# A four-layer graph network on one core: degrees counted inside the sort's pair product, records taken apart within the first convolution, one-hots that read a one from PSUM

## The chip, the cores and the metric

One core of a Trainium2 chip runs the whole program. The metric is the device time of one execution in microseconds (us), as the median of ten runs. Below, PE is the tensor engine (PEld its weight loads), DVE the vector engine, ACT the scalar engine, POOL the GpSimd engine, SP the sync engine, which here only issues transfers. L12 is line 12 of the kernel before.

## The reference, cut to what matters

12,500 nodes with 16 features, 400,000 edges that come sorted by destination in the host's arrays (the kernel sorts them anew, by source and destination bucket). Four layers follow each other, each on `h = relu(layernorm(x))`, and each is added to `x`:

```
deg  = segment_sum(1, dst) + 1 ;  dinv = 1/sqrt(deg)
L0:  two GCN convolutions: out = dinv * (segment_sum((dinv*h)[src], dst) + dinv*h), weights and relu between
L1:  relational messages: W_rel[type[e]] applied to h[src], times an edge score, summed over dst
L2:  edge network: messages from h[src] and 4 edge attributes, summed over dst, divided by max(count, 1), batch norm
L3:  a non-linear coupling of h[src] and h[dst] with the edge weight, summed over src
```

Every layer needs rows gathered by `src` and sums over `dst`. What matters here is how many edges each node has as destination (`deg`), which node of its bucket each edge names (`src & 127`, `dst & 127`), and which type it has.

## The kernel before, in words

**Buckets and groups.** Nodes lie as 98 buckets of 128. The kernel sorts edges into records of 8 words (source low bits, destination low bits, destination bucket and type packed in word 0; edge score, weight, four attributes) so that edges of one (destination bucket, source bucket) pair stand together in granules of G = 9. A group is 128 granules, one a partition; there are NG = 512 groups, of which the first MAIN_S = 396 are in use for these inputs in source order. The rest runs only under a condition (`tc.If` in `in_steps`) that does not hold here.

**Histogram.** One product per 128 edges counts the pairs; from the counts come the start of each pair (`cbase`) and the tables `mvx`, `here`, `spare` from which each granule's place in the destination order (`place`) is made.

**Sort (L455 to L611).** 125 blocks of 3200 edges, 25 columns of 128. For each column: ACT copies the running counts `p_c` to `c_sb` (L573), PE adds this column's pair product, `ohd` by `ohs`, to `p_c` (L574), and PE looks up each edge's start with `ohdt` and `c_sb` (L576, `p_l`). DVE counts equal keys before each edge in its column (L579), picks the edge's own start (L583, L584), and after the 25 columns makes the slots (L589 to L601). POOL scatters the block's 25 columns of records `q` with one indirect transfer each (L603). `q` has two buffers, so a block's `q` is written when the scatter of two blocks before has landed. The degrees have their own products (L475, `count_degrees`): a one-hot `ohl` of the destination's low bits is made after the loop (L586), and the products of `ohd` with it are issued in the next block's program. `ohdt` (L516) is made with `scalar_tensor_tensor` and a column of ones held in PSUM (`fixed`, `one_p`).

**Taking apart (L612 to L690).** After the sort, for all 512 groups: load the records (`rt`, 60 groups at a time), extract source low bits (`slo`), destination low bits (`dl0`), type (`typ`), bucket (`dhi`) on DVE; transpose them on PE and write them as rows to DRAM (`srow`, `trow`, `hrow`, L641 to L660). Then, 35 groups at a time, load `hrow` back to 98 partitions (`hb`), make a one-hot `ht` (L669), multiply with `mvx` (L672), and make `place` with eight small operations (L676 to L687). `dl0` is stored to DRAM and loaded again at L882.

**Convolutions (L889 to L931).** Run twice. Steps of two groups (`in_steps`: `fetch` of one step is issued ahead of `rows` of the step before). Each four groups (LD), `fetch` loads a row block (SP) and makes a one-hot of 4608 columns on DVE (L700, `one_hot_t`: `tensor_scalar` with `is_equal`): in the first convolution the source one-hot `o` from `srow`, which is also stored to `oh_s`; in the second `o` is loaded from `oh_s`, and the type one-hot `ot` from `trow` is made and stored to `oh_t` for layer 1. ACT issues these loads and stores. `rows`: 18 products with the bucket's rows (L919), a copy to `msg` on ACT (L923), in the first convolution a copy of `dl0` beside it on DVE (L925), and two indirect transfers by POOL (L715, `send`), which put each granule in its place of `buf1` or `buf2`. `msg` has six buffers, `o` and `ot` three each, `pg` three. A `sum_pass` in destination order follows each convolution.

**Layer 2 (L1081 to L1115).** Per step: products, a multiplication `q` (L1095) on DVE, a folding of `q` (L1102), and two additions: on POOL `m + q0` (L1104), on DVE `m + q1` (L1105). Then the message is split in three bf16 parts (L245 to L249, ACT and DVE), and POOL sends it.

The order on each engine is fixed when the program is built; an engine takes its instructions in that order.

Of the kernel before, what the change touches and what calls it, by code (L numbers as in the profile page):

```python
# [30 lines left out]
F32 = mybir.dt.float32  # L31
BF16 = mybir.dt.bfloat16
# [12 lines left out]
P = 128  # L45
# [22 lines left out]
LD = 4  # L68
S = UN * G
# [12 lines left out]
def gnn_kernel(  # L82
# [186 lines left out]
    with ExitStack() as begin:  # L269
        base = begin.enter_context(tc.tile_pool(name="base", bufs=1))  # L270
        parts, n = 8, 4
        e1 = base.tile([P, NG * G // parts // n, R], F32, name="e1")
        nc.vector.memset(e1, 0.0)
        nc.vector.memset(e1[:, :, 0:1].bitcast(I32), EMPTY)
        v = rec.rearrange("p (k n s) -> k p n s", k=parts, n=n)
        for k in range(parts):
            nc.scalar.dma_start(v[k], e1.rearrange("p s r -> p (s r)")[:, None, :]
                                .to_broadcast([P, n, NG * G // parts // n * R]))
        w = (NG - MAIN_D) // 4
        for k in range(MAIN_D, NG, w):  # L280
            nc.scalar.dma_start(buf4.rearrange("(p g) c -> p g c", g=NG)[:, k : k + w],
                                zeros[:, None, : G * F].to_broadcast([P, w, G * F]))

        deg_b = base.tile([NB, P], F32, name="deg_b")
        cbase = base.tile([NB, NB], F32, name="cbase")
        mvx = base.tile([NB, NG, 3], BF16, name="mvx")
        n_d = base.tile([P, NB], F32, name="n_d")
        v_d = base.tile([P, NB], F32, name="v_d")
        spare = base.tile([P, NG], F32, name="spare")
        rank_e = base.tile([P, NG], F32, name="rank_e")  # L290
        here = base.tile([P, NG], F32, name="here")
        here_i = base.tile([P, NG], I32, name="here_i")
        nc.gpsimd.iota(here_i, pattern=[[P, NG]], base=0, channel_multiplier=1)
        nc.vector.tensor_copy(here, here_i)

        def one_hot_n(out, v2, n, iota=iota_b):

            nc.vector.tensor_tensor(out.rearrange("p k (m t) -> p k m t", t=2),  # L298
                                    v2[:, :, None, :].to_broadcast([P, v2.shape[1], n // 2, 2]),
                                    iota[:, None, :n].rearrange("p a (m t) -> p a m t", t=2)  # L300
                                    .to_broadcast([P, v2.shape[1], n // 2, 2]), op=ALU.is_equal)


        with tc.tile_pool(name="hist", bufs=2) as hist, tc.tile_pool(name="hpsum", bufs=1, space=PSUM) as ps:
            p_cnt = ps.tile([NB, NB], F32, name="p_cnt")
            clear(p_cnt, NB, NB)
            for it in range(NBE // UE):
                e0 = it * UE * BE
                hi = {}
                for name, idx in (("d", dst), ("s", src)):  # L310
                    v = hist.tile([P, UE, KE], I32, name="v" + name)
                    nc.sync.dma_start(v, idx[e0 : e0 + UE * BE].rearrange("(u p k) -> p u k", u=UE, k=KE))
                    v = v.rearrange("p u k -> p (u k)")
                    t = hist.tile([P, KI], I32, name="t" + name)
                    nc.vector.tensor_scalar(t, v, 7, None, op0=ALU.logical_shift_right)
                    hi[name] = hist.tile([P, KI, 2], BF16, name="hi" + name)
                    nc.vector.tensor_copy(hi[name], t[:, :, None].to_broadcast([P, KI, 2]))
                key = hist.tile([P, KI], F32, name="key")
                nc.vector.scalar_tensor_tensor(key, hi["d"][:, :, 0], float(NB), hi["s"][:, :, 0],
                                               op0=ALU.mult, op1=ALU.add)  # L320
                hd = hist.tile([P, KI], F32, name="hd")
                nc.scalar.copy(hd, hi["d"][:, :, 0])
                for v, row, dt in ((key, keyrow, F32), (hd, drow, BF16)):
                    pt = ps.tile([KI, P], F32, name="pt", bufs=2)
                    nc.tensor.transpose(pt, v, ident)
                    tt = hist.tile([KI, P], dt, name="tt" + row.name[-8:])
                    nc.scalar.copy(tt, pt)
                    nc.sync.dma_start(row[it * KI : (it + 1) * KI, :], tt)
                for u in range(UE):
                    sl = slice(u * KE, (u + 1) * KE)  # L330
                    ohd = hist.tile([P, KE, NB], BF16, name="ohd")
                    one_hot_n(ohd, hi["d"][:, sl, :], NB)
                    ohs = hist.tile([P, KE, NB], BF16, name="ohs")
                    one_hot_n(ohs, hi["s"][:, sl, :], NB)
                    for k in range(KE):
                        nc.tensor.matmul(p_cnt, ohd[:, k, :], ohs[:, k, :], start=False, stop=False,
                                         skip_group_check=True)
            cnt = base.tile([NB, NB], F32, name="cnt")
            nc.vector.tensor_copy(cnt, p_cnt)


        with tc.tile_pool(name="bw", bufs=1) as bw, tc.tile_pool(name="bpsum", bufs=1, space=PSUM) as ps:

            def up(v, shape, by, name):

                f = bw.tile(shape, F32, name=name)
                nc.vector.tensor_scalar(f, v, 1.0 / by, (by - 1) / by - 0.45, op0=ALU.mult, op1=ALU.add)
                nc.vector.tensor_scalar(f, f, MAGIC, MAGIC, op0=ALU.add, op1=ALU.subtract)
                return f

            def up128(v, shape, name):
                i = bw.tile(shape, I32, name=name + "_i")
                nc.vector.tensor_scalar(i, v, float(P - 1), None, op0=ALU.add)
                nc.vector.tensor_scalar(i, i, 7, None, op0=ALU.logical_shift_right)
                f = bw.tile(shape, F32, name=name)
                nc.vector.tensor_copy(f, i)
                return f

            def over_groups(lhsT, v):

                m = lhsT.shape[1]
                p = ps.tile([P, 1024], F32, name="p_g")
                for c in range(0, NG, 512):
                    w = min(512, NG - c)
                    nc.tensor.matmul(p[:m, c : c + w], lhsT, v[:, c : c + w], start=True, stop=True)
                return p[:m, :NG]

            sq = [NB, NB]
            n = up(cnt, sq, G, "n")
            tri = before[:NB, :NB]  # L370
            p_pre = ps.tile(sq, F32, name="p_pre")
            nc.tensor.matmul(p_pre, tri, n, start=True, stop=True)
            p_all = ps.tile(sq, F32, name="p_all")
            nc.tensor.matmul(p_all, ones[:NB, :NB], n, start=True, stop=True)
            tg = up128(p_all, sq, "tg")
            incl = bw.tile(sq, F32, name="incl")
            nc.vector.tensor_tensor_scan(incl, ones[:NB, :NB], tg, 0.0, op0=ALU.mult, op1=ALU.add)
            nc.vector.tensor_sub(incl, incl, tg)
            gs = bw.tile(sq, F32, name="gs")
            nc.vector.scalar_tensor_tensor(gs, incl, float(P), p_pre, op0=ALU.mult, op1=ALU.add)  # L380
            nc.vector.tensor_scalar(cbase, gs, float(G), None, op0=ALU.mult)
            p_ts = ps.tile([NB, 1], F32, name="p_ts")
            nc.tensor.matmul(p_ts, n, ones[:NB, 0:1], start=True, stop=True)
            td = bw.tile([NB, 1], F32, name="td")
            nc.vector.tensor_reduce(td, n, axis=AX.X, op=ALU.add)

            group_i = bw.tile([NB, NG], I32, name="group_i")
            nc.gpsimd.iota(group_i, pattern=[[1, NG]], base=0, channel_multiplier=0)
            group = bw.tile([NB, NG], F32, name="group")
            nc.vector.tensor_copy(group, group_i)  # L390
            ts = bw.tile([NB, 1], F32, name="ts")
            nc.vector.tensor_copy(ts, p_ts)
            first, ends = [], []
            for name, t, bkt in (("s", ts, bkt_s), ("d", td, bkt_d)):
                c = up128(t, [NB, 1], "c" + name)
                p_f = ps.tile([NB, 1], F32, name="p_f", bufs=2)
                nc.tensor.matmul(p_f, tri, c, start=True, stop=True)
# [901 lines left out]
```

## Time and profile before

| what | value |
|---|---|
| median of 10 runs | 11687.88 us (11679.14 to 11690.1) |
| the profiled execution: its own time | 11684.19 us |
| the profiled execution: span, first to last instruction | 11682.2 us |
| busy share of the span | DVE 79%, POOL 67%, PE 59%, PEld 55%, ACT 22% |
| POOL: scatter of the sort, 3125 indirect transfers | 3030.2 us busy, 970 ns each |
| POOL: sends of convolutions and layer 2, 1188 | 1601.6 us busy, 1348 ns each |
| DVE: one-hots of the two convolutions, 2 x 99 | 260.3 + 260.1 us, 2630 ns each |

The program is a sequence of stages with different limits, so a share over the whole span says little; each stage is read by itself. Busy time of POOL for an indirect transfer is the making of its descriptors; the transfer itself runs on the DMA engines afterwards. A "releaser" behind an idle time names what ended the wait. The granted clock of PE is given with each window as a share of full speed.

### The profile page before, as it was taken

The numbers are of one execution on the slowest core, as the hardware profiler recorded it, in microseconds if no ns is written. First come the engines' busy times: TensorE is split into PE (matmuls) and PEld (weight loads), VectorE is DVE, ScalarE is ACT, GpSimd is POOL, SyncE is SP. The second block draws the span as 40 slices with busy tenths as digits, with TensorE's granted clock in tenths as the row PEclk, the third lists the DMA queues.
The fourth block names the chain that finished last, engine by engine and source line by source line (L and its number), as shares of the span: only waits on it lengthen the run. The fifth ranks groups of instructions, "written<-read, shape, count | busy, mean of one in ns | idle before, by whom it ended". The sixth has DMA issues, their size and how long they took to land. (4 is left out here: it accounts for less than half of the span.)

```text
span 11682.2 us, 284671 instructions
## 1 busy us (share of the span) xinstructions
PE 6925.5 (59%) x112895; PEld 6383.5 (55%) x112895; DVE 9234.3 (79%) x17851; ACT 2551.9 (22%) x7316; POOL 7803.4 (67%) x8668
## 2 busy tenths in 40 slices
PE   5655555555555552225622578888867655656776
PEld 5555555555555552224422467777766555546766
DVE  8877877787877775448433899999999788955999
ACT  0122112222112221221222100000046322011555
POOL 0277777777777773884388369999999587300776
PEclk7555555555555555555555589999975799555555
DMA  3344444444444435775488533333334466456443
GB/s 102 96 137 132 132 125 136 137 137 132 132 132 136 137 112 175 238 238 171 125 270 271 167 104 106 103 104 105 101 115 132 122 202 186 152 155 205 138 127 113
DMA packets 1100970, 1704.98 MB, mean 146 GB/s; under 512 B 660792, under 2 KB 727909, under 8 KB 1080779
## 3 DMA queue, kind: packets, MB, share of 16 engines
q1 hardware_dynamic: 746151, 737.61, 21.4%
q10 hardware_dynamic: 164704, 715.37, 18.7%
q0 software_dynamic: 188704, 233.01, 6.3%
q8 instruction: 907, 14.86, 0.5%
q14 instruction: 504, 4.13, 0.1%
HBM read 1079.99 MB, written 555.86 MB: 140 GB/s over the span
## 5 line engine op out<-in xcount | busy, mean ns | idle before, releaser
L603 POOL DMA_INDIRECT rec<-q,slot x3125 | 3030.2, 970 | 1012.9 <-issue 950.7
L576 PE MATMUL p_l<-c_sb,ohdt 98*128 98x98 f32 x6250 | 1875.3, 457 | 242.8 <-DVE gran L591 193.6
L715 POOL DMA_INDIRECT buf<-msg,place x1188 | 1601.6, 1348 | 497.6 <-issue 227.7
L576 PEld LDWEIGHTS p_l<-c_sb,ohdt 98*128 98x128 f32 x6250 | 1634.2, 323 | 323.9 <-issue 318.8
L574 PE MATMUL p_c<-ohs,ohd 128*98 128x98 bf16 x3125 | 817.9, 262 | 1172.8 <-DVE ohs L298 1124.8
L769 DVE TENSOR_TENSOR oh<-lo,row 128x2304 bf16<-128x2304 bf16 x1070 | 1409.4, 1342 | 72.6 <-ACT lo L756 44.1
L1007 PE MATMUL pw<-wt,ot 128*128 128x256 bf16 x10692 | 1235.5, 273 | 263.6 <-DVE pr L1011 244.0
L1007 PEld LDWEIGHTS <-ot 128*128 128x128 fp8e4 x10692 | 1044.8, 98 | 431.3 <-issue 312.5
L574 PEld LDWEIGHTS <-ohd 128*98 128x98 bf16 x3125 | 626.2, 200 | 1134.0 <-DVE ohd L298 971.1
L573 ACT COPY c_sb<-p_c 98x98 f32<-98x98 f32 x3125 | 756.9, 242 | 1488.1 <-PE p_c L574 1476.2
L747 PE MATMUL pg<-xg,o 128*128 128x16 bf16 (+1 forms) x33156 | 947.3, 173 | 204.7 <-DVE o L700 152.5
L747 PEld LDWEIGHTS <-o 128*128 128x128 fp8e4 x33156 | 922.4, 101 | 221.6 <-DVE o L700 164.5
L1011 DVE TENSOR_TENSOR pr<-pw,hg 128x1536 f32<-128x1536 f32 x594 | 1020.2, 1743 | 7.0 <-ACT hg L751 3.9
L919 PE MATMUL pg<-xg,o 128*128 128x48 bf16 x7128 | 324.7, 215 | 1084.4 <-DVE o L700 502.7
L579 DVE SCALAR_TENSOR_TENSOR junk<-keyb,key,fixed 128x128 bf16<-128x128 f32 x3125 | 916.7, 340 | 0.0
L715 POOL DMA_INDIRECT buf<-mm,place x396 | 834.2, 2107 | 121.2 <-issue 67.4
L919 PEld LDWEIGHTS <-o 128*128 128x128 fp8e4 x7128 | 296.6, 118 | 1112.5 <-DVE o L700 524.4
L786 PEld LDWEIGHTS <-oh 128*128 128x128 bf16 x22464 | 652.0, 104 | 432.3 <-DVE oh L769 241.3
L1216 POOL DMA_INDIRECT xj<-buf,place x396 | 396.1, 1000 | 625.4 <-ACT lo L756 539.1
L800 PE MATMUL pa<-m,oh 128*128 128x48 bf16 x11772 | 587.7, 215 | 361.3 <-DVE oh L769 338.8
L1023 DVE TENSOR_TENSOR pr<-pr 128x2304 f32<-128x2304 f32 (+1 forms) x396 | 783.7, 1979 | 0.1
L583 DVE TENSOR_TENSOR own<-p_l,ohs 128x490 f32<-128x490 f32 x625 | 418.1, 669 | 433.7 <-PE p_l L576 429.0
(362 smaller groups left out, 13322.5 us busy)
## 6 DMA issues: line engine op xcount, KB each, us to landing
o<-oh_s ACTq DMA_DIRECT2D x396, 576.0 KB
keyb<-keyrow ACTq DMA_DIRECT2D x125, 1600.0 KB
buf<-zeros SPq DMA_DIRECT2D x120, 1536.0 KB
m<-buf SPq DMA_DIRECT2D x218, 432.0 KB
db<-drow ACTq DMA_DIRECT2D x125, 612.5 KB
mf<-buf SPq DMA_DIRECT2D x109, 576.0 KB
er<-erow SPq DMA_DIRECT2D x109, 576.0 KB
t<-srow SPq DMA_DIRECT2D x99, 576.0 KB
```

The lines of the kernel that those rows point to most:

```text
L573: nc.scalar.copy(c_sb, p_c)
L574: nc.tensor.matmul(p_c, ohd[:, k, :], ohs[:, k, :], start=False, stop=False, skip_group_check=True)
L576: nc.tensor.matmul(p_l[:, k - kb, :], ohdt[:, k * P : (k + 1) * P], c_sb, start=True, stop=True)
L579: nc.vector.scalar_tensor_tensor(junk, keyb[:, k * P : (k + 1) * P], key[:, k : k + 1], earlier_p, op0=ALU.is_equal, op1=ALU.mult, accum_o ...
L603: st = nc.gpsimd.indirect_dma_start(out=rec_rows, out_offset=bass.IndirectOffsetOnAxis(ap=slot[:, k : k + 1], axis=0), in_=q[:, k, :], in_ ...
L715: st = nc.gpsimd.indirect_dma_start(out=buf, out_offset=bass.IndirectOffsetOnAxis(ap=place[:, g : g + 1], axis=0), in_=msg, in_offset=None)
L747: nc.tensor.matmul(pg[:, k, :], o[:, k * P : (k + 1) * P], xg[:, (g + k // G) % LD, c, :], start=c == 0, stop=c == 2)
L769: nc.vector.tensor_tensor(oh.rearrange("p k (m t) -> p k m t", t=2), lo2[:, v : v + S, None, :].to_broadcast([P, S, P // 2, 2]), row[:, No ...
L786: nc.tensor.matmul(pa[:, v + i], oh[:, i * G + k, :], msg[:, i * G + k][:, c], start=k + c == 0, stop=k + c == G + 1)
L1007: nc.tensor.matmul(pw[:, k].rearrange("p i o -> p (i o)"), st["ot"][:, (k0 + k) * P : (k0 + k + 1) * P], wt3[:, c, :], start=c == 0, stop= ...
L1011: nc.vector.tensor_tensor(pr[:, sl], pw, hg[:, sl, :F, None].to_broadcast([P, S // 3, F, F]), op=ALU.mult)
L1023: e.tensor_add(pr[:, :, :n], pr[:, :, :n], pr[:, :, n : 2 * n])
```

## The change

1. **Degrees in the pair product.** `p_c` becomes 226 columns wide; its first 98 are the running pair counts, the other 128 the degrees. `ohs` and the one-hot of the low destination bits lie side by side in one tile `ohm`, and one product per column adds to both. `count_degrees` and `p_deg` are gone. ACT still copies the first 98 columns alone.
2. **Records taken apart within the first convolution.** The stage after the sort is gone, but for the degrees' rsqrt. A generator `take_apart` does the same work for FB = 32 groups, in five pieces with a pause between; `ahead` runs it to the end for groups 0 to 31 when the first convolution starts, and then one piece per `fetch` for the 32 groups that come next. The casts go from DVE to ACT. `dl0` stays in SBUF. Groups from 396 on are taken apart only if they are in use. The pool `base`, which holds the tables, stays open until the end of layer 0.
3. **One-hots with a one in PSUM.** Both convolutions make their one-hots with `scalar_tensor_tensor`, (t == part) * one, where `one` is a column of ones in PSUM. `pg` has two buffers instead of three. The last layer's one-hot (`er`) keeps `tensor_scalar`.
4. **Layer 2:** the addition of L1104 goes from POOL to DVE.

```diff
-            p_c = ps.tile([NB, NB], F32, name="p_c")
-            nc.tensor.matmul(p_c, ident[:NB, :NB], cbase, start=True, stop=False, skip_group_check=True)
-            p_deg = ps.tile([NB, P], F32, name="p_deg")
-            clear(p_deg, NB, P)
+        p_c = ps.tile([NB, NB + P], F32, name="p_c")
+        begin_c = small.tile([NB, NB + P], F32, name="begin_c")
+        nc.vector.memset(begin_c, 0.0)
+        nc.vector.tensor_copy(begin_c[:, :NB], cbase)
+        nc.tensor.matmul(p_c, ident[:NB, :NB], begin_c, start=True, stop=False, skip_group_check=True)
...
-                ohs = sort.tile([P, KE, NB], BF16, name="ohs")
+            ohm = sort.tile([P, KE, NB + P], BF16, name="ohm")
+            ohs = ohm[:, :, :NB]
...
-                count_degrees(degrees)
+            one_hot_n(ohm[:, :, NB:], lo_d, P, iota_p)
...
-                        nc.scalar.copy(c_sb, p_c)
-                        nc.tensor.matmul(p_c, ohd[:, k, :], ohs[:, k, :], start=False, stop=False,
+                    nc.scalar.copy(c_sb, p_c[:, :NB])
+                    nc.tensor.matmul(p_c, ohd[:, k, :], ohm[:, k, :], start=False, stop=False,
...
-                ohl = sort.tile([P, KE, P], BF16, name="ohl")
-                one_hot_n(ohl, lo_d, P, iota_p)
-                degrees = (ohd, ohl)
...
-    def one_hot_t(o, t, np_):
+    def one_hot_t(o, t, np_, one=None):
+        if one is not None:
+            nc.vector.scalar_tensor_tensor(o, t, part[:np_], one[:np_].to_broadcast([np_, LD * GP]),
+                                           op0=ALU.is_equal, op1=ALU.mult, saturate=False)
+            return
         nc.vector.tensor_scalar(o, t, part[:np_], None, op0=ALU.is_equal, saturate=False)
...
+        def take_apart(fin, ps, g0, n):
+            m = n * G
+            c = slice(g0 * G, g0 * G + m)
+            rt = fin.tile([P, FB * G, R], F32, name="rt", bufs=1)
+            nc.sync.dma_start(rt[:, :m], rec_v[:, c])
+            yield
+            w = rt[:, :m, 0].bitcast(I32)
+            typ = fin.tile([P, FB * G], BF16, name="typ")
+            dhi = fin.tile([P, FB], BF16, name="dhi")
+            for by, mask, t in ((0, 255, slo[:, c]), (8, 255, dl0[:, c]), (23, 127, typ[:, :m])):
+                i = fin.tile([P, FB * G], I32, name="fi")
+                nc.vector.tensor_scalar(i[:, :m], w, by, mask, op0=ALU.logical_shift_right, op1=ALU.bitwise_and)
+                nc.scalar.copy(t, i[:, :m])
...
+            yield
...
+            hb = fin.tile([NB, FB * P], BF16, name="hb", bufs=1)
+            nc.sync.dma_start(hb[:, : n * P], hrow[g0 : g0 + n].rearrange("g p -> (g p)")[None, :]
+                              .to_broadcast([NB, n * P]))
+            yield
+            ht = fin.tile([NB, FB * P], BF16, name="ht", bufs=1)
+            nc.vector.tensor_scalar(ht[:, : n * P], hb[:, : n * P], part[:NB], None, op0=ALU.is_equal)
...
+                one = ps.tile([P, 1], F32, name="one", bufs=1)
+                nc.vector.memset(one, 1.0)
+                def ahead(g):
+                    g0, end = (0, MAIN_S) if g < MAIN_S else (MAIN_S, NG)
+                    if (g - g0) % FB == 0:
+                        if g == g0:
+                            for _ in take_apart(fin, ps, g, min(FB, end - g)):
+                                pass
+                        n = min(FB, end - g - FB)
+                        held["ahead"] = take_apart(fin, ps, g + FB, n) if n > 0 else iter(())
+                    next(held["ahead"], None)
                 def fetch(g, st):
                     if g % LD == 0:
+                        if first:
+                            ahead(g)
...
-                            one_hot_t(o, rows_block(rp, srow, g, P, "t"), P)
+                            one_hot_t(o, rows_block(rp, srow, g, P, "t"), P, one)
...
-                            one_hot_t(ot, rows_block(rp, trow, g, REL, "t"), REL)
+                            one_hot_t(ot, rows_block(rp, trow, g, REL, "t"), REL, one)
...
-                nc.gpsimd.tensor_add(m, m, q[:, :, 0, :])
+                nc.vector.tensor_add(m, m, q[:, :, 0, :])
```

## The prediction

> **What bounds the kernel now.** I read first the busy time by stage (columns: busy time and instructions of each engine, then granted clock, DMA share, GB/s):
>
> ```profile
> core 0: us, PE busy (x) PEld busy (x) DVE busy (x) ACT busy (x) POOL busy (x), PEclk, DMA share, GB/s
> 450.00:4460.00 4010.00, 2263.84 (x12501) 2200.74 (x12500) 3135.41 (x11435) 808.93 (x3374) 3030.17 (x3125) 0.51 0.41 131
> 4460.00:4595.00 135.00, 26.61 (x588) 22.18 (x588) 69.53 (x223) 9.76 (x11) 0.39 (x1) 0.50 0.74 254
> 4624.20:5323.20 699.00, 160.92 (x3533) 146.75 (x3529) 279.09 (x292) 172.89 (x197) 578.49 (x396) 0.50 0.72 231
> 5770.00:6468.50 698.50, 160.79 (x3529) 146.87 (x3529) 257.05 (x100) 173.03 (x203) 576.79 (x396) 0.50 0.86 266
> 9196.60:9905.10 708.50, 413.72 (x10454) 393.95 (x10450) 613.46 (x981) 208.91 (x591) 603.64 (x592) 0.98 0.65 196
> ```
>
> In order: the sort; the taking apart of the records; the sends of the first and of the second convolution (first to last send); the sends of the edge network (layer 2). POOL is idle only in the second row. Between the sort's last send (ends 4459.84) and the first convolution's first (4624.23) lie 164 us. Then the groups, by line (busy us, mean ns | idle before):
>
> ```profile
> L603 POOL DMA_INDIRECT rec<-q,slot x3125 | 3030.2, 970 | 1012.9 <-issue 950.7
> L574 PE MATMUL p_c<-ohs,ohd 128*98 128x98 bf16 x3125 | 817.9, 262 | 1172.8 <-DVE ohs L298 1124.8
> L475 PE MATMUL p_deg<-ohl,ohd 128*98 128x128 bf16 x3125 | 352.6, 310 | 308.2 <-DVE ohl L298 308.2
> L700 DVE TENSOR_SCALAR o<-t,part 128x4608 fp8e4<-128x4608 uint8 x99 | 260.3, 2630 | 7.5 <-PE pg L919 4.7 <-DVE msg L925 0.8 <-DMA t<-srow 0.7
> ```
>
> The sort's 3125 sends take 0.97 us and wait only for their own issue (0.30): 25 x 1.27 = 31.8 us a block, and POOL is the bound. The order of time in one block shows how much room the rest has:
>
> ```profile
> 2029.06 2.83 PE L475 MATMUL p_deg<-ohl,ohd 128*98 128x128 bf16 x25 [2.49 <-DVE ohl L298]
> ...
> 2030.30 3.54 DVE L516 SCALAR_TENSOR_TENSOR ohdt<-db,part,fixed 98x3200 f32<-98x3200 bf16 x1
> 2031.40 0.97 POOL L603 DMA_INDIRECT rec<-q,slot  x1 [0.30 <-issue]
> ...
> 2035.71 0.17 DVE L601 SCALAR_TENSOR_TENSOR slot<-s,lane 128x25 int32<-128x25 int32 x1
> ...
> 2039.04 0.97 POOL L603 DMA_INDIRECT rec<-q,slot  x1 [0.30 <-issue]
> 2039.97 0.57 DVE L557 TENSOR_REDUCE q<-pr 128x25 f32<-128x400 f32 x1 [2.92 <-DMA rec<-q,slot]
> ...
> 2044.55 0.26 PE L574 MATMUL p_c<-ohs,ohd 128*98 128x98 bf16 x1
> ...
> 2045.14 0.26 PE L574 MATMUL p_c<-ohs,ohd 128*98 128x98 bf16 x1
> ```
>
> The slots are ready at 2035.88, the first send that reads them starts at 2039.04: about 3 us of room (2.87 in the middle of the stage; 3.9 after block 98, where the spare steps end). The pair products follow each other at 0.593 us, a loop of copy (0.24), product and two hand-overs. In the convolutions POOL is the bound too, for another reason:
>
> ```profile
> 4903.40 0.97 POOL L715 DMA_INDIRECT buf<-msg,place  x1 [0.30 <-issue]
> 4904.68 3.10 POOL L715 DMA_INDIRECT buf<-msg,place  x1 [0.30 <-issue]
> ...
> 4905.05 2.62 DVE L700 TENSOR_SCALAR o<-t,part 128x4608 fp8e4<-128x4608 uint8 x1
> ...
> 4911.49 0.97 POOL L715 DMA_INDIRECT buf<-msg,place  x1 [0.30 <-issue]
> ```
>
> A send that meets a one-hot of L700 ends when the one-hot ends: 3.10 instead of 0.97. In the sort the 3.54 us one-hot of L516, which multiplies by a one that lies in PSUM, leaves the sends that run under it at 0.97. That is the difference the third part uses.
>
> **The change, part by part.** The sum is made against the profiled span, 11682.2.
>
> *Degrees in the pair product.* Removed: 25 products per block (2.83 us on an idle PE) and nothing on the path. Widened: p_c from 98 to 226 columns, inside the loop of 25. No row has 226 columns (the nearest, 256 at 273 ns in L1007, ran at a granted clock of 1.00, the sort at 0.51). Below: 25 products of 128 columns pass in 2.83 us, so 128 columns cost 0.113 us. Above: 98 columns take 262 ns and 128 take 310, 1.6 ns a column, 0.205 us for 128. The second row also holds waits in a burst, so I take 0.11. 24 steps x 0.11 = 2.6 us. The one-hot of the low halves (1.81 us) moves from behind the loop to ahead of it: both places are on the way to the slots, so zero. The reordered small operations cost some 0.2. Room: two blocks run in a loop of last send to free q (1.45 median), q to slots (27.79), slots to send (0.92, from the first block, where POOL waited) and 31.54 of sends, 61.70 against two periods, 63.71: 2.0 us. 2.8 against 2.0 leaves 0.8 per two blocks, 0.4 a block over 96 blocks: **+36** (0 if a little less is lost; with 0.205, 24 x 0.205 + 0.2 - 2.0 = 3.1, halved, x 98, and 1 each in the last 27: +180).
>
> The Trainium skill has a formula for it (TensorE: Matmul & The Clock Gate, Single matmul latency): cold, 219 plus the columns, over 1.2 ns. That gives 264 ns for 98, where the row has 262, and 371 for 226. By it the sort loses about 30; by the steeper row it would be 180, and this is the weightiest number in doubt.
>
> *Records taken apart inside the first convolution.* Removed: the stretch 4460 to 4595, and the store and load of dl0. Added ahead of the first send: records of 32 groups instead of 512. From 4461.4, when the last scatter has landed: in the changed program's order VectorE's layer norm waits for that landing too. Its rows (4594.52 to 4620.04, less three one-hots of 2.61) are 17.7 us; between them now stand six field extractions of about 0.41, a one-hot ht (1.3) and small ones, 4 in all. After these come, still ahead of the first group's places, four one-hots of the new form at 5.0, the first ht's eight small operations (0.2 each) and the second ht: 23. First send 44 us after the landing, about 4506 (25 if the one-hots' waits overlap, 70 if the records' and hrow's loads are late), against 4624. Behind VectorE's new waits (for rt and hb) stand the one-hots and message copies, so PE, ACT and POOL in turn; six message buffers are 12 sends, 15 us of cover, and a load of 1.2 MB is shorter. Without that cover 12 waits of 3 us would be 36.
>
> *One-hots with a one in PSUM.* L516's rate, 3.54 us less about 0.2 for 3200 elements, gives 5.0 us for 4608 instead of 2.63, 198 times. POOL's floor falls to 4 x 1.275 = 5.1 us per four groups from 7.06 (699 / 99), if nothing else holds it. Next in line in the first convolution, per four groups: VectorE 5.0 + two copies of 0.20 + taking apart (3 x 0.41 + 1.3 + 10 x 0.19 = 4.4 over eight steps) = 5.9; DMA 0.72 x 699 / 99 = 5.08 plus 0.74 x 135 us x 396/512 / 99 = 0.78, together 5.86 at a share of 1. Two engines at 5.9 that wait for each other now and then: I take 6.2, so 614 us from the first one-hot at 4483, 8 more to the last send: 5105 against 5323, **-218** (5.9: -248; 6.9: -149). Second convolution: DMA 0.86 x 698.5 / 99 = 6.07, VectorE 5.0. Five windows of 10 us from 5900 have shares of 0.96, 0.78, 0.96, 0.73, 0.95; at 0.95 throughout, 6.39 a step, 633: **-65** (nothing if 0.86 is what these queues reach; -190 if DMA times shrink and POOL's 5.1 is left). pg with two buffers instead of three: PE is busy 161 of 699, zero; 10 if ACT's copies are late.
>
> *Layer 2: one addition from POOL to VectorE.* Here VectorE waits for POOL each step:
>
> ```profile
> 9503.95 0.46 DVE L1105 TENSOR_TENSOR m<-m,q 128x288 f32<-128x288 f32 x1 [0.43 <-POOL m L1104]
> ```
>
> The wait (0.43) goes, one addition of the same form comes, 0.38 from its start to the next (9503.95 to 9504.33): 198 x -0.04 = **-8** (from -40 to +20, the whole 0.46 with a quarter of the waits left). POOL loses 0.80 of its 3.56 per step.
>
> The Trainium skill (SBUF — State Buffer, Who interferes with whom) says that a VectorE instruction with two inputs in SBUF contends with a GpSimd one that reads SBUF. The added one is such. In this stage sends take 1.07 to 1.19 instead of 0.97. By the rule up to 0.46 x 198 = 91 us more on POOL, which has 0.80 a step to spare: still zero on the path.
>
> Sum: +36 - 218 - 65 - 8 = -255, span 11427. The profiled run took 11684.19, 2.0 over its span, and the median 11687.88 lies 3.7 above that: **11433**.
>
> **Rivals.** *DMA is the wall* (0.17): shares stay at 0.86 to 0.87. Then the second convolution gains nothing and the first goes at 5.86 / 0.87 = 6.7 (667 us, -165): 11551. For it: the waits for o<-oh_s and oh_t<-ot in the second convolution (497 and 362 us). Against: ACT, which issues both, is itself held by messages that POOL hasn't sent. *The sort's loop decides* (0.05, slower): 24 steps of D more cost (24 D + 0.2 - 2.0) / 2 a block. At D = 0.30 it is 2.7 x 125 = 337 instead of 36: 11734. It eats the whole gain from D = 0.25 on; the rows reach 0.205. *The one in PSUM does not free POOL* (0.02): one-hots of 5.0 hold a send each, 5.1 + 4.5 = 9.6 a step, 950 us twice, about 12070. Against it stands the send at 2031.40.
>
> **How the numbers follow.** My forecast has 0.73, the rivals 0.17, 0.05, 0.02; 0.03 is left for a loss and a gain that cancel. The forecast's own range, from the ends of its terms, is 11310 to 11500; with the DMA wall 11560. Faster by over 0.2% (23 us, about what a measurement of this kernel can tell): 0.73 + 0.17 + 0.01 of the rest = 0.91; same 0.03; slower 0.06.
>
> **What would show it.** In the sort: pair products 0.70 apart (not 0.59), POOL with a short wait for the slots each block, 32.2 us a block. First send some 45 us after the sort's last. Convolutions' sends at 0.97 throughout, one-hots at 5.0; VectorE near 0.9 busy in the first, DMA share 0.95 in the second. I am wrong if sends keep 3 us, if product steps exceed 0.8, or if VectorE waits for rt or hb more than a few us each.

## The result, and the profile after

The changed kernel takes 13122.68 us (median of 8 runs, 13110.96 to 13136.35) beside 11685.77 for the kernel before (28 runs): a ratio of 1.1229, interval 1.1219 to 1.1239. It is 12% slower, where 2% faster was forecast. The profiled execution took 13122.96 us, with a span of 13121.0.

From here on line numbers of the changed kernel are meant where its profile is shown: L553 and L554 are the two copies into `q`, L569 the count copy `c_sb`, L570 the pair product, L594 the slots, L596 the scatter. Every later run is a kernel of its own, and its lines have that kernel's numbers. First the busy time by stage, as before: the sort, the stretch from its last send to the first convolution's first, the sends of the two convolutions, those of layer 2.

```profile
core 0: us, PE busy (x) PEld busy (x) DVE busy (x) ACT busy (x) POOL busy (x), PEclk, DMA share, GB/s
450.00:6190.00 5740.00, 2182.97 (x9376) 1853.35 (x9375) 3096.99 (x11436) 793.90 (x3374) 3028.16 (x3125) 0.50 0.28 91
6190.00:6237.00 47.00, 10.32 (x192) 8.27 (x193) 40.20 (x44) 13.16 (x27) 1.76 (x2) 0.50 0.66 211
6237.70:6848.10 610.40, 182.55 (x3836) 160.61 (x3833) 521.59 (x449) 184.95 (x289) 394.81 (x396) 0.50 0.93 299
7297.30:7943.80 646.50, 160.81 (x3528) 147.11 (x3525) 486.58 (x100) 169.93 (x202) 384.94 (x396) 0.50 0.92 288
10673.90:11352.10 678.20, 407.24 (x10455) 387.36 (x10451) 672.97 (x1178) 209.39 (x592) 388.11 (x396) 0.99 0.68 205
```

Everything behind the sort did roughly what was forecast: the stretch of 164 us is 47, the convolutions fell from 699 and 698.5 to 610 and 646.5, layer 2 from 708.5 to 678. The sort alone grew from 4010 to 5740 us, and no engine worked more in it: POOL's 3028 us are the 3030 of before. The groups say the same (busy, mean ns of one, idle before them):

```profile
L596 POOL DMA_INDIRECT rec<-q,slot x3125 | 3028.5, 969 | 2744.5 <-issue 2675.4
L570 PE MATMUL p_c<-ohm,ohd 128*98 128x226 bf16 x3125 | 1086.7, 348 | 2809.8 <-ACT c_sb L569 1947.5
```

Sends still take 0.97 us, but POOL now stands idle 2744.5 us ahead of them, 1732 more than before. (The profile names nothing that ended this wait; "issue" stands for that.) The wide pair product takes 348 ns instead of 262, and what it waits for is new: the count copy on ACT. The waits of ACT in the sort, kernel before first, changed kernel second (us in total, times, longest):

```profile
ACT q L558 <- DMA rec<-q,slot: 1673.7, 123, 15.3
ACT c_sb L573 <- PE p_c L574: 1432.7, 3030, 3.9
```

```profile
ACT c_sb L569 <- PE p_c L570: 2915.5, 2938, 14.1
ACT q L553 <- DMA rec<-q,slot: 1949.3, 123, 22.2
```

The wait of 1949.3 us for the landings isn't new: it was there before, with 1673.7. What changed is what stands behind it. One block in order of time:

```profile
2542.03 0.24 ACT L569 COPY c_sb<-p_c 98x98 f32<-98x98 f32 x1 [0.44 <-PE p_c L570]
...
2542.33 0.35 PE L570 MATMUL p_c<-ohm,ohd 128*98 128x226 bf16 x1
...
2556.18 0.97 POOL L596 DMA_INDIRECT rec<-q,slot  x1 [0.30 <-issue]
2558.61 0.24 ACT L553 COPY q<-wv 128x25 f32<-128x25 f32 x1 [16.33 <-DMA rec<-q,slot]
2558.73 0.29 ACT L554 COPY q<-a 128x100 f32<-128x100 f32 x1
...
2558.90 0.23 ACT L569 COPY c_sb<-p_c 98x98 f32<-98x98 f32 x1
2559.19 0.35 PE L570 MATMUL p_c<-ohm,ohd 128*98 128x226 bf16 x1 [16.11 <-ACT c_sb L569]
...
2563.25 0.35 PE L570 MATMUL p_c<-ohm,ohd 128*98 128x226 bf16 x1
...
2571.49 0.18 DVE L594 SCALAR_TENSOR_TENSOR slot<-s,lane 128x25 int32<-128x25 int32 x1
...
2572.41 0.97 POOL L596 DMA_INDIRECT rec<-q,slot  x1 [15.26 <-issue]
```

The products run up to 2542.33 and stop. ACT's next instruction is a copy into the next block's `q`, which waits until the scatter now going through POOL has landed. Its last send ends at 2557.15, the copy starts 1.5 us later, and only then come the block's last count copies (7 of its 25, 4.7 us to the end of the last product), the picking and the slots (8.8 to the first send). POOL, which was to run without a pause, waits 15.26 us ahead of this block (14.5 in the median of all blocks): the period, from one block's first send to the next block's, is 46.20 us instead of 31.85 (blocks 3 to 97).

The built order of ScalarE's instructions shows it without any time (kernel before, changed kernel; "x24" is a run of equal instructions):

```
before:   c_sb  c_sb x24  q<-wv  q<-a  keyb  db  c_sb  c_sb x24  q<-wv  q<-a  keyb  db ...
changed:  c_sb  c_sb x17  q<-wv  q<-a  c_sb x7  keyb  db  c_sb  c_sb x18  q<-wv  q<-a  c_sb x6 ...
```

In the program text the copies into `q` stand ahead of their own block's columns in both kernels. Which place they get among the columns of the block before is decided when the program is built. In the kernel before all 25 count copies of a block are out ahead of them; in the changed one 4 to 7 (7 in 60 blocks, 6 in 38) still stand behind. Why the builder chose so isn't known.

### The profile page after: what moved, and what is told of

Same layout as the page of the kernel before. It is cut to its first block, busy times and chain, and to the rows that moved or that the text cites. A ratio compares the mean times of both kernels' runs of the same rounds, so it can differ in the third digit from the quotient of the medians.

```text
span 13121.0 us, 277786 instructions
## 1 busy us (share of the span) xinstructions
PE 6844.6 (52%) x109663; PEld 6030.4 (46%) x109663; DVE 9682.0 (74%) x18013; ACT 2546.5 (19%) x7420; POOL 7209.5 (55%) x8470
## 5 line engine op out<-in xcount | busy, mean ns | idle before, releaser
L596 POOL DMA_INDIRECT rec<-q,slot x3125 | 3028.5, 969 | 2744.5 <-issue 2675.4
L572 PEld LDWEIGHTS p_l<-c_sb,ohdt 98*128 98x128 f32 x6250 | 1570.9, 312 | 2987.5 <-issue 2734.9
L570 PE MATMUL p_c<-ohm,ohd 128*98 128x226 bf16 x3125 | 1086.7, 348 | 2809.8 <-ACT c_sb L569 1947.5
L579 DVE TENSOR_TENSOR own<-p_l,ohm 128x490 f32<-128x490 f32 x625 | 418.1, 669 | 2589.6 <-PE p_l L572 2589.6
L572 PE MATMUL p_l<-c_sb,ohdt 98*128 98x98 f32 x6250 | 1918.8, 411 | 722.1 <-DVE gran L584 596.7
L639 POOL DMA_INDIRECT buf<-msg,place x1188 | 1168.0, 983 | 1042.3 <-ACT msg L926 349.9
L569 ACT COPY c_sb<-p_c 98x98 f32<-98x98 f32 x3125 | 755.6, 242 | 2960.8 <-PE p_c L570 2947.1
L570 PEld LDWEIGHTS <-ohd 128*98 128x98 bf16 x3125 | 629.2, 201 | 874.0 <-DVE ohd L299 494.7
L671 PEld LDWEIGHTS <-o 128*128 128x128 fp8e4 x33156 | 922.2, 101 | 213.2 <-DVE o L624 165.9
L710 PEld LDWEIGHTS <-oh 128*128 128x128 bf16 x22464 | 651.9, 104 | 433.9 <-DVE oh L693 240.0
L724 PEld LDWEIGHTS <-oh 128*128 128x128 bf16 x11772 | 503.8, 117 | 437.2 <-DVE oh L693 427.4
```

Source lines behind the costliest of these rows:

```text
L569: nc.scalar.copy(c_sb, p_c[:, :NB])
L570: nc.tensor.matmul(p_c, ohd[:, k, :], ohm[:, k, :], start=False, stop=False, skip_group_check=True)
L572: nc.tensor.matmul(p_l[:, k - kb, :], ohdt[:, k * P : (k + 1) * P], c_sb, start=True, stop=True)
L596: st = nc.gpsimd.indirect_dma_start(out=rec_rows, out_offset=bass.IndirectOffsetOnAxis(ap=slot[:, k : k + 1], axis=0), in_=q[:, k, :], in_ ...
L639: st = nc.gpsimd.indirect_dma_start(out=buf, out_offset=bass.IndirectOffsetOnAxis(ap=place[:, g : g + 1], axis=0), in_=msg, in_offset=None)
L671: nc.tensor.matmul(pg[:, k, :], o[:, k * P : (k + 1) * P], xg[:, (g + k // G) % LD, c, :], start=c == 0, stop=c == 2)
```

## The experiments

Two theories are told apart. The **order theory**: the loss comes from count copies standing behind copies that wait for a scatter. The **width theory**: it comes from the product of 226 columns, which is what the prediction had held to be the weightiest number in doubt.

### Order mended; product narrowed

The first run keeps the wide product and puts the copies into `q` behind the last count copy; the second leaves 128 columns out of the product and so counts no degrees, and the builder then gives ScalarE the old order by itself.

```diff
+        last_c = None
...
+            with tc.issue_after(last_c.ins) if last_c else ExitStack():
-            nc.scalar.copy(q[:, :, 2], wv)
-            nc.scalar.copy(q[:, :, 3:7], a4)
+                nc.scalar.copy(q[:, :, 2], wv)
+                nc.scalar.copy(q[:, :, 3:7], a4)
...
-                    nc.scalar.copy(c_sb, p_c[:, :NB])
+                    last_c = nc.scalar.copy(c_sb, p_c[:, :NB])
```

> The changed kernel with one edit: each block's two copies into q on ScalarE stand behind the last of the block before's 25 count copies (c_sb), no longer among them. Order theory: the sort's loss comes from the last 4 to 7 count copies of each block standing behind the copies into q, which wait for the landing of the last scatter but one. Then the stall of about 16 us in each block's chain of products goes, the period of a block falls from 46.2 us to 31.9 to 32.2, the sort's stage from 5740 to about 4020 to 4060, and the whole to 11390 to 11440 us. Width theory: the loss comes from the pair product of 226 columns. Product and q buffers are unchanged, so the whole stays at 13090 to 13130 us.

```diff
-                    nc.tensor.matmul(p_c, ohd[:, k, :], ohm[:, k, :], start=False, stop=False,
+                    nc.tensor.matmul(p_c[:, :NB], ohd[:, k, :], ohs[:, k, :], start=False, stop=False,
```

> The changed kernel with the 128 degree columns left out of the pair product (the degrees are not counted, all else is done). In the built order the copies into q then stand behind all 25 count copies, as before the change, so this run has both differences at once and is read against the run with the order alone. Order theory: the pair products stand 0.593 us apart instead of 0.677, the period is 31.85 us, the whole 11380 to 11400 us, and the run with 226 columns and mended order is no more than 40 us above it. Width theory: this run is 1700 us under the other.

The mended order takes 11407.95 us (ratio to the kernel before 0.9761, interval 0.9745 to 0.9778), the narrow product 11383.83 (0.9740, 0.9720 to 0.9759). The order theory holds: 1715 us go with the place of two copies, and 24 are left for the width. Up to the last block of the sort the changed kernel and the mended one have the same order of tiles and operations on PE and POOL, and on DVE in all but 44 of 11913 places, so the first run differs in ScalarE's order and in little else. (The narrow one differs from the mended one on DVE as well, so the 24 are not the width's alone.) Four windows of the mended order, sort, both convolutions and layer 2, ACT's wait in the sort, and one block's end on ACT in order of time:

```profile
450.00:4478.40 4028.40, 2179.51 (x9375) 1851.50 (x9374) 3119.48 (x11435) 793.63 (x3374) 3030.41 (x3125) 0.50 0.41 130
4525.20:5134.70 609.50, 182.55 (x3837) 160.08 (x3833) 520.41 (x449) 184.92 (x289) 394.43 (x396) 0.50 0.94 299
5583.80:6224.50 640.70, 161.23 (x3528) 147.23 (x3525) 487.18 (x100) 169.98 (x202) 385.01 (x396) 0.50 0.93 290
8954.40:9632.60 678.20, 405.80 (x10454) 385.81 (x10450) 672.92 (x1178) 209.37 (x592) 388.12 (x396) 0.99 0.68 205
```

```profile
ACT q L555 <- DMA rec<-q,slot: 1298.6, 123, 22.5
```

```profile
2393.53 0.24 ACT L571 COPY c_sb<-p_c 98x98 f32<-98x98 f32 x1 [0.44 <-PE p_c L572]
2404.16 0.24 ACT L555 COPY q<-wv 128x25 f32<-128x25 f32 x1 [10.38 <-DMA rec<-q,slot]
2404.28 0.29 ACT L556 COPY q<-a 128x100 f32<-128x100 f32 x1
...
2404.45 0.23 ACT L571 COPY c_sb<-p_c 98x98 f32<-98x98 f32 x1
```

The sort's last send ends at 4478.4 instead of 6190.4. The same instruction still waits 1298.6 us for the same landings, now at next to no cost: all 25 count copies of the block in hand are ahead of it. POOL waits over 1 us ahead of a block's first send 3 times in 124, where it did so 122 times in the changed kernel. The period is 31.93 us, products 0.678 apart.

### The order of after put into the kernel before

If the place is the cause, it must do the same harm to the old product. The copies into the next block's `q` (and their loads) are issued by hand behind column 17, or 8, of the current block, in the kernel before.

```diff
+            def early(blk):
...
+                tc.keep_in_program_order(nc.scalar.copy(q[:, :, 2], wv))
+                tc.keep_in_program_order(nc.scalar.copy(q[:, :, 3:7], a4))
+                return q
...
-                nc.scalar.copy(q[:, :, 2], wv)
-                nc.scalar.copy(q[:, :, 3:7], a4)
...
+                        if k == 17 and blk + 1 < NBE:
+                            ready[blk + 1] = early(blk + 1)
-                        nc.scalar.copy(c_sb, p_c)
+                        tc.keep_in_program_order(nc.scalar.copy(c_sb, p_c))
```

> The kernel before the change, its product of 98 columns untouched, with the next block's two copies into q put behind column 17 of the current block on ScalarE, so that 8 count copies stand behind them. Order theory: a block's period becomes landing 1.6 + copies 0.4 + 8 x 0.593 + last products to slots 6.9 + slots to send 0.75 + sends 31.5 = 45.9 us instead of 31.85, 14.05 x 123 = 1730 us more, the whole about 13415 us (13300 to 13500). Width theory: nothing changes, 11680 to 11700 us.

> As the run before, with the copies into q behind column 8, so that 17 count copies stand behind them. Order theory: 9 x 0.593 = 5.3 us more a block than with column 17, a period of 51.2 us, 656 us more than that run, the whole about 14070 us (13950 to 14150). Width theory: 11680 to 11700 us.

With column 17: 13461.61 us (1.1517, 1.1494 to 1.1540), a period of 46.40. With column 8: 14524.24 (1.2426, 1.2402 to 1.2451). The copies with column 17, on ACT:

```profile
2041.72 0.24 ACT L505 COPY q<-wv 128x25 f32<-128x25 f32 x1 [29.27 <-DMA rec<-q,slot]
2041.84 0.29 ACT L506 COPY q<-a 128x100 f32<-128x100 f32 x1
2042.02 0.23 ACT L584 COPY c_sb<-p_c 98x98 f32<-98x98 f32 x1
```

The first run is as expected to 0.4%; of the second the direction is right, but the expected size is 454 us short and the time lies outside its range: the period is 55.0 and not 51.2. Its trace has an explanation, which no run tested: a 3.54 us one-hot, that of the next block but one, now runs on DVE ahead of the last sum of the picks, L595 (with column 17 it runs behind the slots).

```profile
3754.40 3.54 DVE L529 SCALAR_TENSOR_TENSOR ohdt<-db,part,fixed 98x3200 f32<-98x3200 bf16 x1
3757.85 0.66 DVE L595 TENSOR_REDUCE slot_f<-own 128x5 f32<-128x490 f32 x1
```

So an edit that moves instructions on one engine can change the built order of another too, and the price per column moved was 0.95 us (8.6 us of period for 9 columns), not the 0.593 of a product. In both runs DVE also makes a later block's `ohd` and `ohs` (1.40 and 1.43 us) ahead of the slots, where the kernel before makes them behind. So these two runs show the harm in the old product, but not of the place alone; that rests on the mended order.

### A third buffer for q, the other parts alone, layer 2 alone

The next two sets ran on chips on which the kernel before itself took 14130.85 and 14252.02 us. There a part of the sort is held by something else (last section), so these runs are compared within their set alone.

```diff
-            q = sort.tile([P, KE, R], F32, name="q")
+            q = sort.tile([P, KE, R], F32, name="q", bufs=3)
```

> The changed kernel with three buffers for q and nothing said of the order. In the built order each block's copies into q then stand even further ahead, behind the first count copy of the block before, and 24 of its count copies stand behind them. The place alone would make this the worst of all (a period over 54 us, 14400 us); but the landing that they wait for is now that of the scatter one block earlier, done some 20 us before. Order theory in its full form (a place among the count copies and a release that is late): no stall, 11380 to 11410 us. If the place alone costs: 14000 us or more; if the width costs: 13100 us.

> The changed kernel with the copies into q behind the block's last count copy and three buffers for q instead of two, so that no block's slots wait for the landing of the last scatter but one. Order theory: the period is POOL's 31.54 of sends and a short hand-over, 31.8 us instead of 31.93, 0.13 x 125 = 16 us less than with the order alone: 11392 us (11380 to 11400). If the loop through q's buffers was not what still holds the period in the mended order: 11408.

With three buffers and the order left to the builder 13710.90 us (0.9704, 0.9685 to 0.9723), with three buffers and the mended order 13666.71 (0.9678, 0.9662 to 0.9694). The absolute times can't be held against the forecasts. What can be read: in the first, 24 of 25 count copies stand behind copies into `q`, and it is only 44 us from the second. But for one in the first run's opening blocks, none of ACT's waits in the sort is for a landing of `rec` (in the first the copies into `q` still wait 749 us in all, which the profile puts down to DVE). So on this chip a place among the count copies cost 44 us at most where the release came early, which fits a loss that needs both, the place and a late release. As these blocks are held by something else as well, at 49.8 and 49.3 us each, more of a cost could be hidden.

```diff
-            ohm = sort.tile([P, KE, NB + P], BF16, name="ohm")
-            ohs = ohm[:, :, :NB]
+            ohs = sort.tile([P, KE, NB], BF16, name="ohs")
...
+            count_degrees(degrees)
```

> The changed kernel with the sort of before (98 columns in the pair product, degrees counted by 25 products of their own): only the taking apart, the one in PSUM and layer 2's addition are changed. The two traces differ outside the sort by 117 us up to the first send, 89 and 52 in the convolutions and 30 in layer 2, 288 in all. If these parts don't depend on the sort: 11688 - 288 = 11400 us (11380 to 11415), and the degrees in the pair product, in the mended order (11408), are worth 8 us of loss (-10 to +30). If some of the 288 belongs to the sort's change (the degrees being ready with the sort's end): 11430 or more, and the degrees' part would be a gain.

```diff
-                nc.vector.tensor_add(m, m, q[:, :, 0, :])
+                nc.gpsimd.tensor_add(m, m, q[:, :, 0, :])
```

> The sort of before, the taking apart and the one in PSUM as in the first run of this set, but layer 2's addition left on POOL as before the change. The difference to that run is what the addition is worth. Prediction's term: 8 us (-20 to +40). The two traces' stages: 30 us. So 11400 + 30 = 11430 us if the trace's difference is the addition's, 11408 by the prediction's working; below 11400 if the addition on VectorE costs by contention.

The sort of before with the other parts: 13935.26 (0.9860, 0.9843 to 0.9876). The same with layer 2's addition on POOL: 13951.67 (0.9875, 0.9858 to 0.9891), 16 us more. Neither forecast in us can be judged here, so these kernels, and the one with three buffers and the mended order, were run again, and met another such chip:

> The same kernel as e5_convs, again, because in that set the kernel before itself took 14131 us, with count copies up to 7 us late on ScalarE within each block of the sort, which no run of the first set shows. Where the kernel before takes 11688: 11400 us (11380 to 11415) if the other parts don't depend on the sort's change; then the degrees in the pair product, order mended (11408), cost 8 us (-10 to +30). 11430 or more if part of the 288 us gained outside the sort belongs to the degrees.

> The same kernel as e1b_order_q3, again, for the same reason. Where the kernel before takes 11688: 11392 us (11380 to 11400) if the loop through q's two buffers is what still holds the period at 31.93 in the mended order, 11408 if not.

> The same kernel as e8_l2pool, again, for the same reason. In the set on the slow chip it took 16 us more than the run with the addition on VectorE. Where the kernel before takes 11688: 8 us more than that run by the prediction's term, 16 by the first set, 30 if the whole difference of the two traces' layer 2 is the addition's.

In this order they took 14086.70 (0.9885, 0.9869 to 0.9902), 13803.45 (0.9689, 0.9673 to 0.9705) and 14086.43 us (0.9879, 0.9863 to 0.9896). Beside the kernel before of their sets the later parts alone gain 196 and 165 us; the 288 that the stages add up to are neither confirmed nor refuted where the kernel before takes 11688. In both sets the mended order with three buffers is some 2% ahead of the old sort with the same later parts; whether it also beats 11407.95 where the kernel before takes 11688 wasn't settled. The addition of layer 2 is worth 16 us in one set and 0 in the other: inconclusive. The sends change all the same: their mean in that stage is 1126 ns with the addition on POOL and 979 and 976 on DVE. The stage, first to last send, takes 708.0 and 708.7 us with the addition on POOL, 691.7 and 710.6 on DVE.

### The one in SBUF instead of PSUM

This kernel has the mended order too; the edit shown is against that one.

```diff
-                one = ps.tile([P, 1], F32, name="one", bufs=1)
-                nc.vector.memset(one, 1.0)
+                one = ones[:, 0:1]
```

> The changed kernel with the copies into q behind the last count copy (11408 us), and in the convolutions the one read from SBUF instead of PSUM; the form of the instruction is the same. If the operand's place in PSUM is what leaves POOL free: a send that meets a one-hot is held for its rest again, 1.4 us and more on average instead of 0.97 to 1.00, one-hots of 2.6 to 5.0 us hold one send each in 198 steps, and the two convolutions take 140 us (one-hots of 2.6) to 650 us (one-hots of 5.0) more: 11550 to 12060 us. If the three-operand form alone frees POOL, whatever its operands' place: 11408 (11395 to 11420).

14249.36 us in the second of these sets (0.9991, 0.9980 to 1.0002), read by stages beside the run of that set with mended order and three buffers (13803.45), which has the one in PSUM: the convolutions' sends take 919.0 and 908.6 us instead of 662.7 and 680.3. Their windows, with the one in SBUF and in PSUM:

```profile
6736.10:7655.10 919.00, 183.11 (x3836) 159.25 (x3833) 527.42 (x449) 192.14 (x289) 796.58 (x396) 0.50 0.60 198
8104.40:9013.00 908.60, 170.40 (x3527) 152.98 (x3525) 487.37 (x99) 171.41 (x201) 785.06 (x396) 0.50 0.69 205
```

```profile
6741.70:7404.40 662.70, 197.38 (x3838) 168.78 (x3834) 523.55 (x449) 189.06 (x289) 391.33 (x396) 0.50 0.86 275
7853.60:8533.90 680.30, 163.83 (x3528) 148.51 (x3525) 484.08 (x98) 169.67 (x201) 384.08 (x396) 0.50 0.90 273
```

In the time order of the first convolution with the one in SBUF:

```profile
6949.79 0.97 POOL L641 DMA_INDIRECT buf<-msg,place  x1 [0.30 <-issue]
...
6950.19 5.02 DVE L623 SCALAR_TENSOR_TENSOR o<-t,part,ones 128x4608 fp8e4<-128x4608 uint8 x1
...
6951.06 4.98 POOL L641 DMA_INDIRECT buf<-msg,place  x1 [0.30 <-DMA buf<-msg,place]
...
6956.35 0.97 POOL L641 DMA_INDIRECT buf<-msg,place  x1 [0.31 <-issue]
```

The one-hot is as long as with PSUM (5.01 us), but a send that starts beneath it is held for 4.98 us; 99 and 97 sends of 396 are over 1.2 us, where the other run has 13 and none. It is the operand's place in PSUM that leaves POOL free, and with the one in SBUF the two stages take 256 and 228 us more, 484 together, within the 140 to 650 that were expected. The Trainium skill (SBUF — State Buffer, Who interferes with whom) says that a VectorE instruction with two inputs in SBUF contends with a GpSimd one that reads SBUF: these rows agree, with 4.98 against 0.97 us, if a send counts as one that reads SBUF.

## Why the prediction was wrong, by its own steps

**The step that failed** is the sort's term, +36 us, and in it the half sentence "the reordered small operations cost some 0.2". Of the built order the prediction speaks for VectorE alone. On ScalarE the same change moved two copies, which wait for a landing, ahead of 4 to 7 count copies of nearly every block. The sort's last send came 1730.5 us later (6190.4 instead of 4459.8), and 1712.0 of these are gone in the run with the mended order (4478.4). The prediction had this loop in hand, "last send to free q (1.45 median), q to slots", with a room of 2.0 us; but it took freeing `q` to delay the start of the next block but one, never a column in the midst of the block itself. With the copies in the midst the part of a block behind them can't lie beneath the sends of the block before: the period grew by 14.35 us a block where 0.4 had been allowed. None of the three signs under "I am wrong if" came (sends at 0.97, product steps of 0.677, VectorE's waits for `hb` 2.8 us each); the sign that failed is the 32.2 us a block.

**The slower rival** named the right place, "the sort's loop decides", with the wrong mechanism: it was priced by the wider product (24 D), with an upper end of +180 from the steepest row. The price was right and small: products stand 0.678 us apart instead of 0.593, D = 0.085 where 0.11 was taken. In the mended order the sort ends 18.6 us later than before, against the +36, and 8.3 of these lie ahead of its first send; the period rose by 0.08 us, where 0.4 was allowed. The Trainium skill's formula (TensorE: Matmul & The Clock Gate, Single matmul latency) makes 107 ns of the 128 columns; the product's own rows rose by 86 (262 to 348), at a granted clock of 0.50.

**The sum of the rest was right.** In the run with mended order, beside the span of before: -117.6 for the stretch after the sort and -89.5 in the first convolution (-207 together; -218 was forecast), -57.8 in the second (-65), -30.3 in layer 2 (-8), with the sort's +18.6 and -2.3 elsewhere a span of 11403.3 against 11682.2. The forecast of 11433 is 25 us from that kernel's 11407.95, partly by luck: layer 2 gave 22 us more than forecast, the convolutions 18 less. In the changed kernel DVE is 0.85 busy in the first convolution and the DMA share 0.93, so it is near both limits, as argued; the first send comes 47 us after the sort's last, where some 45 was forecast.

**Layer 2** is a mis-sized term. The working took the wait of 0.43 us to be exchanged for an addition; the sends of that stage also became shorter, from 1127 to 980 ns. The isolating runs reproduce the shorter sends but not the 30 us, so what these are worth stays open; on the chip of the first set the stage takes 708.1 us in the run with column 17, whose addition is on POOL, and 678.2 with the mended order, and nothing else in the text of that layer differs. The up to 91 us more on POOL, which the prediction drew from the Trainium skill's rule on two inputs in SBUF (SBUF — State Buffer, Who interferes with whom), are not there: in the changed kernel 360 of the 396 sends overlap the added addition (441 ns) and take 0.96 us. In the kernel before nearly all overlap other instructions of DVE, at 1.07 or 1.19 us; which of these lengthens them wasn't tested.

**The two other rivals** fell: the DMA share rose from 0.86 to 0.92 in the second convolution (no wall at 0.86), and the sends of the convolutions, with one-hots that read PSUM, stay at 0.97 to 1.00 in the mean, while the run with SBUF shows that the fear behind the third rival (some 950 us a stage) was the right one for the wrong operand (919 and 909).

**Slips of the working** that don't bear on the failure: the stated range of 11310 to 11500 is narrower than the ends of its terms, which add up to 11210 to 11739; the product step that eats the whole gain is D = 0.27 by the prediction's own formula, not 0.25; and by the skill's formula the sort's loss comes to 37 us and not 30.

## What to carry to other kernels

Where a builder fixes each engine's order, compare the built order of every engine before and after an edit, and look for an instruction with a far-off release (a buffer that a transfer must free) that has slipped ahead of a loop's short hand-overs. The total of a wait says little of its price: 1674, 1299 and 1949 us of the same wait cost next to nothing, next to nothing and some 1715, by what was queued behind it. Pin such an instruction behind the loop, or give it the buffer that ends its wait (the buffer alone was measured only on a chip where the sort was held by something else too).

## What the runs showed of the hardware, unexpected

On the chips of the second and third set, the engines that wait for PE go on late while a scatter runs. From the run with the old sort and the other parts, whose sort has the same order on every engine as that of the kernel before; ACT alone, where "remote" marks a wait whose end the profile puts down to no instruction:

```profile
3538.11 0.24 ACT L576 COPY c_sb<-p_c 98x98 f32<-98x98 f32 x1 [2.60 <-remote]
3540.94 0.24 ACT L576 COPY c_sb<-p_c 98x98 f32<-98x98 f32 x1 [2.58 <-remote]
3545.86 0.24 ACT L576 COPY c_sb<-p_c 98x98 f32<-98x98 f32 x1 [4.67 <-remote]
3552.86 0.24 ACT L576 COPY c_sb<-p_c 98x98 f32<-98x98 f32 x1 [6.76 <-remote]
```

Worked out over blocks 10 to 114 of the trace: from the end of a pair product to the next count copy pass 0.04 us in the first 8 us after a block's first send, 6.5 us between 20 and 28, at most 7.2, and 0.04 again from 32 on (medians). The way back, from the copy to the product, stays at 0.05 in the median; DVE, which waits for PE's lookups, is up to 6.7 us late too. In the trace of the kernel before, whose execution took 11684.19 us, the same hand-over never takes more than 0.09. The DMA engines are nearly idle then: between 3531 and 3557 their share is 0.03. A block takes 51.6 us there instead of 31.85. Instructions themselves are no slower (sends 966 ns there, 970 before; the product of 98 columns 253 and 262). The profile models the ends of matrix products, so whether the signals are late or the products' own ends can't be told, and what holds them wasn't found.
